# Dropped places and weights of the last lists, place by place on ScalarE

## The chip, the cores and the metric

The kernel runs on one core of a Trainium2 chip. The metric is the device time of one execution in microseconds, as the median of several runs. A core has five engines that run their own instruction queues and wait for one another by semaphores: TensorE (PE, with its weight load PEld), VectorE (DVE), ScalarE (ACT), GpSimd (POOL) and SyncE (SP). Here POOL does little else than issue indirect DMAs (gathers and scatters of rows), and SP issues the plain DMAs.

## The reference, cut to what matters

Sixteen graphs of 1024 nodes with 64 channels each, and a weighted adjacency matrix for each graph. Layer 0 is a dense product; layer 1 takes, for every node and channel, three quantiles over the node's neighbours:

```python
# layer 0
h = relu(layernorm(x));  x = x + matmul(adj / clip(sum(adj, 2), 1), h)
# layer 1
h = relu(layernorm(x))
adj_d = _dilate_adj(adj, mask)      # nodes with over 10 neighbours lose every (m+1)//2-th one,
                                    # in both directions of the edge
vals = where(adj_d > 0, h of the neighbour, big);  sv = sort(vals, axis=2);  m = number of valid ones
for tau, wt in zip([0.25, 0.5, 0.75], [0.25, 0.5, 0.25]):
    pos = tau * (m - 1)             # linear interpolation between floor(pos) and ceil(pos)
    agg += wt * (sv[floor(pos)] * (1 - frac) + sv[ceil(pos)] * frac)
out = h + agg
x = x + (relu(out @ W1 + b1) @ W2 + b2) * mask
```

The three quantiles together are a weighted sum over sorted places: each place k has one weight per node, which depends on m alone.

## The kernel before, in words

**Lists.** The kernel does not sort 1024 values for a node. It lists each node's neighbours (`listing`, `endings`), sorts the nodes by their number of neighbours into tiles of 128, and writes their records in that order to a table in DRAM (`srt`). The graphs are taken in four groups of four. In a group the tiles of equal list length form classes: 15, 10, 8, 7 (two tiles), 6, 5 (four), 4 (four), 3 (six), 2 (six) and 1 (five) neighbours (`CAPS`). A class is one `Job` with `n` places (the node itself is the first) and `T` tiles; with 15, 10, 8 and 6 neighbours `T` is 1. The longest lists of all graphs go into four jobs of 88, 28, 21 and 18 neighbours (`long_lists`); the first of them has the tag `l0` and is sorted in blocks as its gathers arrive.

**A job.** `Job.run` has POOL gather row by row: for place k an indirect DMA brings, for 128 nodes, the neighbour's 64 values and two marks into `A[:, k, t, :]` (tile `places`, or `lplaces` for a long list). Then `sort` works on VectorE. It compares the marks with the node's number (`rem`), which gives `gone`, 1 where the edge was dropped; from the keys and `gone` it gets `ok` and the number of valid neighbours, and from that the distances of the places from the three quantile positions (`counts`: `valid`, `q`, `u`, shown as `wu`). The values of gone neighbours are raised by 1e30, so that they sort behind all others:

```python
nc.vector.scalar_tensor_tensor(vals, gone..., HUGE, vals, op0=OP.mult, op1=OP.add)   # the drop
```

ScalarE then turns `u` into weights (`steps`: Abs, then Relu). `passes` does the sorting network: min and max of places, written to one of two copies, `A` (copy 0) or `other` (copy 1: PSUM for the short lists, tile `lother` in SBUF for the long ones). The last part is `weigh`: `w` is the sum of the three weights, and the sorted places are multiplied by it, into the tile `prod` for the short lists, in place for the long ones. `layers` then has PE add up the weighted places (matmuls with the identity into `pt`), ScalarE copy the sum out (`ot`), and PE, ScalarE and PE do W1, Relu (`hid`) and W2; VectorE adds the residual (`y`), and POOL scatters `y` to the output.

**Order.** The order on VectorE and POOL, and so on all engines, is fixed when the program is built. The steps are generators that yield an engine and a time from which they may go on; `Plan` keeps a clock for each engine with a price for every instruction, and always takes the step that may begin first, by its rank. `SLACK`, `LOOSE` and `LATE` are added to the times at which a result is thought to be there. `later` puts the passes of a list behind others while enough gathers are queued. So an edit of one step can move all later ones. Tiles have few buffers: 4 of `places`, 2 of `prod`, 1 of `other` and `lother`, 3 of `lplaces`. All planned instructions are recorded at one line, L240, so the rows of the profile are told apart by their tiles.

The edit lies in `sort` and `weigh`; `counts`, `steps`, `passes` and `layers` are as they were.

Of the kernel before, what the change touches and what calls it, by code (L numbers as in the profile page):

```python
# [14 lines left out]
AF = mybir.ActivationFunctionType  # L15
OP = mybir.AluOpType
AX = mybir.AxisListType

P = 128
# [4 lines left out]
HUGE = 1.0e30  # L24
# [57 lines left out]
def runs_of(left):  # L82

    left, runs = sorted(left), []
    while left:
        best = left[:1]
        for s in sorted({x - left[0] for x in left[1:]}):
            run = left[:1]
            while run[-1] + s in left:
                run.append(run[-1] + s)  # L90
            if len(run) > len(best):
                best = run
        runs.append((best[0], best[1] - best[0] if len(best) > 1 else 1, len(best), 1, 1))
        left = [x for x in left if x not in best]
    return runs
# [131 lines left out]
SLACK = 2.0  # L227
# [18 lines left out]
class Plan:  # L246
# [25 lines left out]
    def room(self, name, bufs):  # L272

        tiles = self.slots.get(name, ())
        if len(tiles) < bufs:
            return 0.0
        old = tiles[-bufs]
        return INF if self.users[old] else max(self.used.get(old, 0.0), self.ready.get(old, 0.0))

    def at(self, *tiles):  # L280
        return max(self.ready.get(t.tensor.name, INF) for t in tiles)
# [67 lines left out]
def kernel(  # L349
# [27 lines left out]
    with tc.manual_schedule(engines={mybir.EngineType.DVE, mybir.EngineType.Pool}):  # L377
        list_path(tc, x, adj, nodemask, w1, b1, w2, b2, out, go)
# [7 lines left out]
def list_path(ctx, tc, x, adj, nodemask, w1, b1, w2, b2, out, go):  # L386
    nc = tc.nc
    B, N, C = x.shape
# [5 lines left out]
    NG = len(GROUPS)  # L394
# [115 lines left out]
    plan = Plan(nc)  # L510
    plan.parts.update(tab.tensor.name for tab in tabs)
    nc = plan.nc
    new, free, room, at = plan.tile, plan.release, plan.room, plan.at
    always = lambda: 0.0
# [330 lines left out]
    class Job:  # L845
# [121 lines left out]
        def places(self, copy, run, shift=0):  # L967
            first, d1, n1, d2, n2 = run
            first += shift
            if copy == 2:  # L970
                return self.S[:, :, :C].unsqueeze(1)
            src = self.A if copy == 0 else self.other
            if n2 == 1:
                return src[:, first:first + d1 * (n1 - 1) + 1:d1, :, :C]
            one = src[:, first, 0, :C]
            row = src.shape[3]
            return bass.AP(
                tensor=one.tensor, offset=one.offset,
                ap=[one.ap[0], [d2 * row, n2], [d1 * row, n1], one.ap[1]],
            )  # L980
# [43 lines left out]
        def steps(self):  # L1024
            nc.scalar.activation(self.u, self.u, AF.Abs)
            nc.scalar.activation(self.u, self.u, AF.Relu, bias=wt0, scale=-QUANTILES[0][1])

        def merge(self):
            self.counts(self.ok)
            yield "ACT", lambda: at(self.u) + SLACK  # L1030
            self.steps()
            yield "DVE", always, self.later
            yield from self.passes(len(self.ops) - 1, self.landed)
            yield from self.weigh()

        def sort(self):
            n, T, pool, short, A, S = self.n, self.T, self.pool, self.short, self.A, self.S
            name, bufs = self.tag, self.bufs1
            rem = new(pool, [P, n - 1, T, 2], F32, name + "rem2", bufs)
            nc.vector.tensor_tensor(  # L1040
                rem, A[:, 1:, :, C:],
                self.node.unsqueeze(1).unsqueeze(3).to_broadcast([P, n - 1, T, 2]), OP.is_equal,
            )
            gone = new(pool, [P, n - 1, T], F32, name + "gone", bufs, users=1)
            nc.vector.tensor_tensor(gone, rem[:, :, :, 0], rem[:, :, :, 1], OP.max)
            ok = new(pool, [P, n - 1, T], F32, name + "ok", bufs)
            nc.vector.scalar_tensor_tensor(
                ok, self.keys.rearrange("p t k -> p k t"), 0.0, gone, op0=OP.is_gt,
                op1=OP.subtract,
            )  # L1050
            self.ops, self.count, self.copies = network(n, T * C, one=T == 1)
            self.counts(ok)

            vals = A[:, 1:, :, :].rearrange("p k t w -> p (k t) w")[:, :, :C]
            nc.vector.scalar_tensor_tensor(
                vals,
                gone.rearrange("p k t -> p (k t)").unsqueeze(2).to_broadcast(
                    [P, (n - 1) * T, C]
                ),
                HUGE, vals, op0=OP.mult, op1=OP.add,  # L1060
            )
            free(gone)
            yield "ACT", lambda: at(self.u) + SLACK
            self.steps()
            yield "DVE", lambda: max(
                room("prod", 2) if short else 0.0,
                room(name + "other", 1),
            ), self.later
            if short:
                Bt = self.Bt = new(ps_o, [P, 3 * HALF], F32, "other", 1, users=1)  # L1070
                self.other = Bt[:, :n * T * C].rearrange("p (k t c) -> p k t c", k=n, t=T)
            else:
                self.other = self.Bt = new(pool, [P, n, T, C], F32, name + "other", 1, users=1)
            self.done = {}
            yield from self.passes(0, plan.clock["DVE"])
            yield from self.weigh()

        def weigh(self):
            n, T, pool, short, A, S = self.n, self.T, self.pool, self.short, self.A, self.S
            name, bufs, Bt = self.tag, self.bufs1, self.Bt  # L1080
            u, count, copies, places = self.u, self.count, self.copies, self.places
            yield "DVE", lambda: at(u) + SLACK, self.later

            w = new(pool, [P, count, T], F32, name + "w", bufs)
            nc.vector.tensor_tensor(w, u[:, 0, :, :], u[:, 1, :, :], OP.add)
            nc.vector.scalar_tensor_tensor(w, u[:, 2, :, :], 2.0, w, op0=OP.mult, op1=OP.add)
            free(u)

            total = max(count + 1, 4)
            prod = None  # L1090
            if short:
                prod = new(pool, [P, T, total, C], F32, "prod", 2, users=1)
                if count + 1 < total:
                    nc.vector.memset(prod[:, :, count + 1:, :], 0.0)

            for copy in (1, 0):
                mine = [k for k in range(count) if copies[k] == copy]
                for run in runs_of(mine):
                    first, step, number = run[:3]
                    sl = slice(first, first + step * (number - 1) + 1, step)  # L1100
                    src = places(copy, run)
                    nc.vector.tensor_tensor(
                        prod[:, :, sl, :].rearrange("p t k c -> p k t c") if short else src, src,
                        w[:, sl, :].unsqueeze(3).to_broadcast([P, number, T, C]), OP.mult,
                    )
            if short:
                free(A)
                free(Bt)
                yield "ACT", lambda: at(S)
                nc.scalar.copy(prod[:, :, count, :], S[:, :, :C])  # L1110
                free(S)

                terms = [
                    [prod[:, t, k:min(k + 2, total), :].rearrange("p k c -> p (k c)")
                     for k in (0, *range(4, total, 2), 2)]
                    for t in range(T)
                ]
                plan.add(self.layers(terms, [prod]), self.urgent)
            else:
                terms = [[places(copies[k], (k, 1, 1, 1, 1))[:, 0, 0, :] for k in range(count)]  # L1120
                         + [S[:, 0, :C]]]
                plan.add(self.layers(terms, [A, Bt]), -1000)
# [354 lines left out]
    nc = tc.nc  # L1477
# [291 lines left out]
```

## Time and profile before

| what | value |
|---|---|
| median of 3 runs | 1457.18 us (1456.25 to 1458.25) |
| profiled execution | 1457.89 us, its span 1456.0 us |
| VectorE busy | 1214.5 us, 83% of the span |
| GpSimd busy | 960.6 us, 66% |
| TensorE busy | 745.0 us, 51%, at a mean granted clock of 0.703 |
| ScalarE busy | 579.9 us, 40% |
| DMA | 132.20 MB, 91 GB/s on average |

The profile is of one execution. The span runs from its first to its last instruction. A row names the line, the engine, the operation, and the tiles written and read; shapes are partitions x elements. "idle before" is the time that the engine stood still just ahead of the row, with what ended it; "issue" means that nothing which the profile shows was waited for. The first two thirds (up to about 950 us) are layer 0 and the first groups' lists, in which all engines have work. After that come the last group's lists and the long ones.

### The profile page before, as it was taken

Reading aid. Unit: us, or ns where it says so; the run is one execution under the profiler, and the core shown is the slowest. Engines: PE = TensorE matmul, PEld = TensorE weight load, DVE = VectorE, ACT = ScalarE, POOL = GpSimd, SP = SyncE. Lnnn points to the kernel's source line nnn. Section 1 sums busy time; section 2 is a strip of 40 time slices with the busy share of each in tenths; the row PEclk is TensorE's granted clock in tenths of the full one; section 3 lists DMA queues with packets and bytes.
Section 4 is the critical chain, followed back from the end, with each engine's and each line's share of the span. In section 5 each row is a group of like instructions: output and inputs, shape, how many; then the busy total and the mean of one; then the engine's idle time right before and its main releaser. Section 6 shows DMA issues by size and latency. Waiting matters only on the chain.

```text
span 1456.0 us, 14752 instructions
## 1 busy us (share of the span) xinstructions
PE 745.0 (51%) x3186; PEld 463.6 (32%) x3186; DVE 1214.5 (83%) x4039; ACT 579.9 (40%) x1747; POOL 960.6 (66%) x1120
## 2 busy tenths in 40 slices
PE   4777877345697566783666660002300262134674
PEld 2434434223345434352443430001200141134453
DVE  6868798997989968899766874868999979999885
ACT  7989978444656527672353830000000010001110
POOL 0132227777767887677778576577777877777754
PEclk9879998668697687895587775555555575558576
DMA  5445567524464416472232334121111111212100
GB/s 183 138 128 184 176 199 203 137 52 143 100 175 117 107 34 181 121 191 78 71 108 76 87 70 89 42 55 44 37 23 24 27 29 27 41 34 46 24 16 14
DMA packets 134589, 132.20 MB, mean 91 GB/s; under 512 B 100196, under 2 KB 102884, under 8 KB 134372
## 3 DMA queue, kind: packets, MB, share of 16 engines
q1 hardware_dynamic: 102972, 91.00, 21.8%
q0 software_dynamic: 31520, 40.19, 12.8%
q8 instruction: 27, 0.44, 0.1%
q14 instruction: 70, 0.57, 0.1%
HBM read 111.62 MB, written 23.61 MB: 93 GB/s over the span
## 4 chain that ended last, share of the span: by engine, by line
DVE 36%; POOL 22%; issue 11%; PE 10%; DMA 10%; ACT 9%; SPq 0%; DVEq 0%; POOLq 0%; ACTq 0%
POOL places L240 14%; DVE places L240 6%; PE ps_small L240 5%; PE pt L240 5%; DMA at<-in_adj_dram 5%; DVE lplaces L240 4%; DVE other L240 4%; DVE rec L240 4%; DMA places<-tab,idx 3%; POOL out_dram L240 3%; ACT sg L240 3%; DVE l0other L240 3%; POOL lplaces L240 2%; ACT ln_sq L240 2%; DVE sg L240 2%
## 5 line engine op out<-in xcount | busy, mean ns | idle before, releaser
L240 POOL DMA_INDIRECT places<-tab,idx x372 | 375.5, 1009 | 114.5 <-issue 106.7
L240 PE MATMUL pt<-ident,prod 128*128 128x128 f32 (+1 forms) x736 | 162.0, 383 | 389.8 <-DVE prod L240 325.0
L240 PE MATMUL ps_small<-att,h 128*65 128x512 f32 x512 | 254.3, 644 | 27.9 <-ACT att L240 9.4
L240 PEld LDWEIGHTS pt<-ident,prod 128*128 128x128 f32 (+1 forms) x736 | 131.6, 264 | 422.2 <-issue 250.6
L240 POOL DMA_INDIRECT srt<-row,to x128 | 130.3, 1018 | 179.4 <-ACT row L240 158.6
L240 PE MATMUL pt<-ident,at 128*128 128x128 f32 x1024 | 168.4, 309 | 65.9 <-ACT att L240 51.8
L240 DVE MAX8 rec<-sg 128x8 f16<-128x256 f16 x512 | 180.1, 414 | 4.4
L240 POOL DMA_INDIRECT lplaces<-whole,lidx x125 | 145.4, 1164 | 38.1 <-issue 36.9
L240 ACT ACTIVATE sg<-at 128x1024 f16<-128x1024 f32 x128 | 134.9, 1054 | 87.0 <-DMA at<-in_adj_dram 75.1
L240 PEld LDWEIGHTS pt<-ident,at 128*128 128x128 f32 x1024 | 130.0, 158 | 113.8 <-ACT att L240 77.6
L240 POOL DMA_INDIRECT places<-tab,last_idx x124 | 133.5, 1077 | 37.8 <-issue 35.7
L240 ACT ACTIVATE wu<-wu 128x39 f32<-128x39 f32 (+9 forms) x40 | 9.4, 235 | 354.2 <-DVE wu L240 354.0
L240 ACT COPY att<-pt 128x512 f32<-128x512 f32 x256 | 142.0, 583 | 18.9 <-PE pt L240 16.9
L240 DVE TENSOR_TENSOR sg<-sg,keyed 128x1024 f16<-128x1024 f16 x128 | 87.3, 682 | 48.3 <-ACT sg L240 48.3
L240 PEld LDWEIGHTS ps_small<-att,h 128*65 128x65 f32 x512 | 73.8, 150 | 164.5 <-issue 122.7
L240 ACT COPY ot<-pt 128x128 f32<-128x128 f32 (+3 forms) x56 | 22.4, 400 | 220.5 <-PE pt L240 220.4
L240 POOL DMA_INDIRECT out_dram<-y,nodes_i x93 | 94.0, 1010 | 22.3 <-issue 13.3
L240 PE MATMUL ps_small<-ot,w_sb 128*128 128x128 f32 (+3 forms) x112 | 50.8, 544 | 29.5 <-ACT ot L240 16.0
L240 DVE TENSOR_TENSOR places<-places,other 128x128 f32<-128x128 f32 (+6 forms) x160 | 56.3, 354 | 3.3
L240 PE MATMUL ps_small<-w_sb,hid 128*128 128x64 f32 x256 | 51.8, 343 | 7.1 <-ACT hid L240 6.8
L240 ACT ACTIVATE hid<-ps_small,b_sb 128x128 f32<-128x128 f32 (+2 forms) x56 | 28.2, 504 | 64.0 <-PE ps_small L240 63.9
L240 DVE TENSOR_TENSOR places<-other,places 128x128 f32<-128x128 f32 (+5 forms) x136 | 48.7, 365 | 1.7
(270 smaller groups left out, 1635.3 us busy)
## 6 DMA issues: line engine op xcount, KB each, us to landing
at<-in_adj_dram SPq DMA_DIRECT2D x128, 512.0 KB
places<-tab,idx POOLq DMA_INDIRECT x372, 2.6
whole<-tab SPq DMA_DIRECT2D x4, 1057.0 KB
tab<-row SPq DMA_DIRECT2D x16, 264.0 KB
xt<-in_x_dram SPq DMA_DIRECT2D x16, 256.0 KB
srt<-row,to POOLq DMA_INDIRECT x128, 3.4
lplaces<-whole,lidx POOLq DMA_INDIRECT x125, 2.5
places<-tab,last_idx POOLq DMA_INDIRECT x124, 2.5
```

Source lines behind the costliest of these rows:

```text
L240: ins = getattr(self._engine, op)(*args, **kwargs)
```

## The change

A new method, `helped`, says for a job whether ScalarE is to take part: jobs of the last group and the long lists other than the 88-place one, with one tile, where the planner's clock of ScalarE is less than 2 us ahead of VectorE's. For such a job the drop is done on ScalarE: `gone` is multiplied by 1e30, and each place gets its column of `gone` as a bias. In `weigh` each place that is to be weighted by copy 0 (for the long lists by both copies) is multiplied on ScalarE by its column of `w`. Both yield to the planner after every four places. The first pass of such a list waits for `A` plus `SLACK`.

```diff
+        def helped(self):
+            return (
+                self.g >= NG - 1 and self.tag != "l0" and self.T == 1
+                and plan.clock["ACT"] < plan.clock["DVE"] + 2.0
+            )
@@ sort
-            vals = A[:, 1:, :, :].rearrange("p k t w -> p (k t) w")[:, :, :C]
-            nc.vector.scalar_tensor_tensor(
-                vals,
-                gone.rearrange("p k t -> p (k t)").unsqueeze(2).to_broadcast(
-                    [P, (n - 1) * T, C]
-                ),
-                HUGE, vals, op0=OP.mult, op1=OP.add,
-            )
+            helped = self.helped()
+            if helped:
+                yield "ACT", lambda: at(gone) + SLACK
+                nc.scalar.mul(gone, gone, HUGE)
+                for t in range(T):
+                    for k in range(1, n):
+                        if (t or k > 1) and k % 4 == 1:
+                            yield "ACT", always
+                        val = A[:, k, t, :C]
+                        nc.scalar.activation(val, val, AF.Identity, bias=gone[:, k - 1, t:t + 1])
+            else:
...
             yield "DVE", lambda: max(
-                room("prod", 2) if short else 0.0,
+                at(A) + SLACK if helped else 0.0, room("prod", 2) if short else 0.0,
                 room(name + "other", 1),
             ), self.later
@@ weigh
+            helped = self.helped()
             for copy in (1, 0):
                 mine = [k for k in range(count) if copies[k] == copy]
+                if helped and (copy == 0 or not short):
+                    yield "ACT", lambda: at(w) + SLACK
+                    for e, k in enumerate(mine):
+                        if e and e % 4 == 0:
+                            yield "ACT", always
+                        for t in range(T):
+                            src = places(copy, (k, 1, 1, 1, 1))[:, 0, t, :]
+                            nc.scalar.activation(
+                                prod[:, t, k, :] if short else src, src, AF.Copy,
+                                scale=w[:, k, t:t + 1],
+                            )
+                    continue
...
-                yield "ACT", lambda: at(S)
+                if not helped:
+                    yield "ACT", lambda: at(S)
                 nc.scalar.copy(prod[:, :, count, :], S[:, :, :C])
```

More of the change, by code (lines that the diff above doesn't have):

```diff
@@ L1052, in sort @@
             self.counts(ok)
-            vals = A[:, 1:, :, :].rearrange("p k t w -> p (k t) w")[:, :, :C]
-            nc.vector.scalar_tensor_tensor(
-                vals,
-                gone.rearrange("p k t -> p (k t)").unsqueeze(2).to_broadcast(
-                    [P, (n - 1) * T, C]
-                ),
-                HUGE, vals, op0=OP.mult, op1=OP.add,
-            )
+            helped = self.helped()
[9 more added lines that the diff above has]
+            else:
+                vals = A[:, 1:, :, :].rearrange("p k t w -> p (k t) w")[:, :, :C]
+                nc.vector.scalar_tensor_tensor(
+                    vals,
+                    gone.rearrange("p k t -> p (k t)").unsqueeze(2).to_broadcast(
+                        [P, (n - 1) * T, C]
+                    ),
+                    HUGE, vals, op0=OP.mult, op1=OP.add,
+                )
             free(gone)
@@ L1094, in weigh @@
                     nc.vector.memset(prod[:, :, count + 1:, :], 0.0)
+            helped = self.helped()
             for copy in (1, 0):
                 mine = [k for k in range(count) if copies[k] == copy]
+                if helped and (copy == 0 or not short):
[8 more added lines that the diff above has]
+                                scale=w[:, k, t:t + 1],
+                            )
+                    continue
                 for run in runs_of(mine):
```

## The prediction

> **What bounds the kernel now.** I read the page's busy line, then the busy time by stretch, then who waited for whom on VectorE from 1151 us on, then the chain that ended last, and last the timeline of the final 22 us. 1151.3 us is where the first edited instruction starts (the 28-place drop below); the changed program's order is the same before it.
>
> ```profile
> PE 745.0 (51%) x3186; PEld 463.6 (32%) x3186; DVE 1214.5 (83%) x4039; ACT 579.9 (40%) x1747; POOL 960.6 (66%) x1120
> ```
>
> The 40% of ScalarE (ACT) is an average over two halves. By stretch (columns: span, then PE, PE load, DVE, ACT, POOL busy, granted clock, DMA share, GB/s):
>
> ```profile
> 1200.00:1250.00 50.00, 11.42 (x42) 9.30 (x41) 47.62 (x158) 3.01 (x11) 38.56 (x53) 0.51 0.16 32
> 1300.00:1350.00 50.00, 25.88 (x182) 23.29 (x181) 46.95 (x120) 4.04 (x11) 39.61 (x37) 0.74 0.21 38
> 1383.20:1440.50 57.30, 35.93 (x202) 27.68 (x202) 52.07 (x190) 7.61 (x18) 31.89 (x55) 0.74 0.05 17
> ```
>
> In the stage that is edited, VectorE (DVE) is at 94 to 95%, ScalarE at 6 to 13%. POOL's 39 of 50 us are gathers of 0.95 us with 0.30 us of issue between them, so POOL is full as well until its last gather ends at 1383.2. What VectorE waited for from 1151 us on:
>
> ```profile
> DVE rem L240 <- DMA places<-tab,idx: 9.5, 1, 9.5
> DVE y L240 <- PE ps_small L240: 6.7, 1, 6.7
> DVE rem L240 <- issue: 6.4, 3, 3.9
> DVE prod L240 <- PE pt L240: 3.5, 1, 3.5
> DVE rem L240 <- DMA places<-tab,last_idx: 0.6, 2, 0.3
> ```
>
> That is 20.0 us before the last list's weights (9.5 + 6.4 + 3.5 + 0.6) and 6.7 us after. All `rem` rows are waits for a gathered list, so two clocks run here: POOL's gathers, and VectorE's own queue. After 1385 the gathers are over and VectorE works off the long lists alone. The chain that ended last closes so:
>
> ```profile
> 1418.75 1.62 DVE y L240 x8
> 1435.67 1.25 DVE lplaces L240 x5
> 1440.39 5.12 PE pt L240 x32
> ```
>
> And the last list on VectorE (start, duration, instruction, idle before):
>
> ```profile
> 1438.70 0.17 DVE L240 TENSOR_TENSOR lw<-lwu 128x15 f32<-128x15 f32 x1
> ...
> 1439.11 1.09 DVE L240 TENSOR_TENSOR lother<-lother,lw 128x896 f32<-128x896 f32 x1
> 1440.12 0.21 DVE L240 TENSOR_TENSOR lplaces<-lplaces,lw 128x64 f32<-128x64 f32 x1
> ...
> 1447.26 0.28 DVE L240 SCALAR_TENSOR_TENSOR y<-ps_small,lS 128x64 f32<-128x64 f32 x1 [6.73 <-PE ps_small L240]
> ```
>
> From the weights' start at 1438.70 to `y` at 1447.26 is 8.56 us, of it 6.87 from PE's first matmul. The span then ends 8.7 us after `y`, with the output scatter at 1447.83.
>
> [...] `ln_sq`, 64 elements with one pointer, has 340 ns; five `h` with two pointers (433 ns each) take 1.77 us, so the step is (1.77 - 0.43) / 4 = 0.335, an overlap of 0.10. One pointer at 64 elements is thus 0.24 us a step (estimate). [...] the trace has two table loads, and no Identity. [...]
>
> **What is removed.** All seven candidate lists take the branch in the built program, at both places. From the groups kept apart by shape, drops: 28, 21, 18 places (long) 2.017, 1.550, 1.351; 15, 10, 8, 6 places 1.150, 0.817, 0.684, 0.549; sum 8.12. Weights: long 1.552 + 0.226, 1.291, 1.092 + 0.215; short 1.026 (13 places) and 0.215; sum 5.62. Fourteen instructions, 13.74 us of durations. In a full queue one starts about 0.08 before its forerunner ends (the 1.09 us one at 1439.11 is followed at 1440.12), so 13.74 - 14 x 0.08 = 12.6 us of VectorE's time go.
>
> **What is added.** On ScalarE 7 multiplies of `gone` (about 0.2), 106 drops and 68 weights: 174 x 0.24 + 1.4 = 43 us over 305 us in which ScalarE was busy 31. There is room. But it has to be in time. A drop of 15 places ends 0.4 + 0.2 + 15 x 0.24 = 4.2 us after its `rem`. Summing the old rows' times along VectorE's new order, the first comparison on that list stands 8.6 us of work after its `rem`; for the lists of 10, 8 and 6 places it is 15.9, 18.7 and 7.0 us against 3.0, 2.5 and 2.0; for the long ones over 45 us against at most 7.4. So no drop is waited for, and I price them at nothing; without that cover each costs its 2 to 7 us. `gone` itself, `wu` and the evictions (`ot`, `hid`) wait behind up to 28 drops, 6.7 us; each `y` on VectorE is placed later than that, by 5 us where it is tightest (the 12-place and 18-place lists' `y`, ahead of the last long list).
>
> **What moves.** The planner re-sorts every queue after 1151 us. POOL has the same instructions, but nine scatters (some 1.31 us each with their memset) now stand ahead of parts of the last list's five gathers, and its last gather is 16 instructions later. From the end of the 12-place list at 1376.0: five scatters 6.5, four gathers 5.1, four scatters 5.2, one gather: issued 1393.1, ended 1394.1, landed (1.8 later, as 1383.24 to 1384.97) at 1395.9, where it was 1385.0. The other lists' last gathers hold their places to within two instructions, so they land when they did (the eight-place list's come 32 earlier). SP issues the same small loads.
>
> Now VectorE against the landings, in sums of old durations from 1151.3 in the new order. The old `rem` of the five-place list came after 20.1 us of work, the new after 20.4: it waits 9.4 to 1181.1. Next, 15 places: work 38.3, ready 1199.0, landed 1200.9, wait 1.9. 10, 8, 14 and 6 places (51.8, 65.2, 108.4, 118.2): ready after landing. 20 places: 147.2, ready 1309.8 against about 1311, wait 1.2. 16 places: none. 18 places: 192.6, ready 1356.4 against 1359.45, wait 3.1. 12 places: 209.2, ready 1376.1 against 1377.9, wait 1.7. Last five places: 227.6, ready 1396.2 against 1395.9: none. Waits 17.3 instead of 20.0: the removed work partly becomes waiting for gathers (18 and 20 places), while the 3.5 us for `prod` should go, since its new place is some 8 us behind PE's last read. The last list's weights start after 253.0 us of work instead of 265.8 (11.4 removed before them, 1.35 us of `y` now stand after): 1151.3 + 253.0 + 17.3 = 1421.6; the same sum for before gives 1437.1 against the true 1438.7, small gaps I don't list, of which the landings absorb most; I take 1421.9. That is 16.8 earlier.
>
> The end gets longer. PE reads the `lplaces` term first, and ScalarE scales it last of 15: two sums 0.41, hand-over 0.1, 15 x 0.24 + 0.1 = 3.7, hand-over 0.1, PE to `y` 6.87, and another list's matmul put among these 0.4: 11.6 instead of 8.56, +3.0. `y` at 1433.5, its scatter at 1434; POOL's eight queued scatters from 1422 on end at about 1433, just ahead. Sum: -16.8 + 3.0 = -13.8. The profiled execution is 1457.89 us with a span of 1456.0; it would be 1444.1. Against the median of 1457.18 that is 1443.4; I say 1443.5.
>
> **Unknowns, both ends.** The ScalarE step: 0.24, at best 0.21 (`row<-rec`, 32 elements), at worst 0.43 with no overlap: -0.5 to +2.9 us at the end. Landings of the last five-place list: -1 to +6 (POOL mean gather 1.39, not 1.25, with its long ones). The `prod` and `y` waits: 0 to 4.
>
> **Rivals.** (A) as summed, -12 to -17: 0.68. (B) POOL's moved scatters become the wait: one of them stands at the queue's head for its `y`, and the last gathers land 5 us later still, VectorE waits at the last `rem` and ends later by the same; or PE's `prod` wait stays (3.5). For it: POOL is full. Against: those `y` are on VectorE by 1370, their scatters due at 1382 or later. -7 to -10, about 1449: 0.22. (C) Slower: the small ScalarE instructions cost far more than their rows, for instance a table load (1.28 us in this trace) at each change of function. At the end alone 15 x (p - 0.24) must exceed 13.8: it decides from p = 1.16 us. Against it: the built program has two table loads, as before. At 1.5 us a piece the end is 19 us longer, 1462: 0.04. (D) The gain is refilled by waits for gathers, nothing is left, 1457: for it, 9.5 of 20 us of waits are of this kind; against, after 1385 there are no gathers, and 55 us of VectorE's queue remain: 0.03. The rest, 0.03, is a gain over 17.
>
> **Numbers.** Likeliest 1443.5, its own range 1440 to 1446; with B's centre 1440 to 1450.5. Within 0.2% (2.9 us) is about what a measurement of this kernel can tell from no change. Faster 0.93 (A, B and the rest), same 0.03 (D), slower 0.04 (C).
>
> **What would show it.** Right: VectorE's busy time down by 13 to 14 us, ScalarE's up by about 174 x 0.34 = 60; seven `gone` rows on ScalarE, no third table load; no new VectorE wait for ScalarE; the last `lw` at about 1422 and PE's last run of 32 starting some 4.5 us after it. Wrong: VectorE waiting on `lplaces`, `places` or `y` from ScalarE or PE by more than 4 us, or a last `rem` after 1400.

## The result, and the profile after

The changed kernel takes 1442.55 us (median of four, 1442.01 to 1443.08), the kernel before 1457.41 us (median of four): a ratio of 0.9899, with a 95% interval of 0.9881 to 0.9916. The prediction was 1443.5 us. The profiled execution has a span of 1440.1 us where it was 1456.0, so 15.9 us less, and its own time is 1442.01 us. That profiled pair differs by 1.0 us more than the medians do. The twelve runs of the experiments below were measured in three groups, each with its own runs of the kernel before, which takes 1821 to 1834 us there, with engines standing still for reasons that no view names. The record names the chips of the groups as 0, 3 and 15, and none for the measurement above. I say "the normal chip" and "these chips" for short; whether the chip makes the difference, or something else, isn't known. Total times are compared only inside one group, and what is read from a trace is said each time. The ratios of these groups are made from the faster runs of both kernels alone (in the second group 9 of the 63 of the kernel before), so they aren't the quotients of the medians beside them, which are of all runs.

The busy line of the page:

```profile
PE 744.5 (52%) x3186; PEld 464.1 (32%) x3186; DVE 1202.7 (84%) x4025; ACT 621.0 (43%) x1928; POOL 958.0 (67%) x1118
```

VectorE has 14 instructions and 11.8 us less, ScalarE 181 instructions and 41.1 us more. The busy time by stretch, in the two stretches shown of before (columns: span, then PE, PE load, DVE, ACT, POOL busy, granted clock, DMA share, GB/s):

```profile
1200.00:1250.00 50.00, 11.77 (x42) 9.39 (x42) 48.00 (x169) 13.51 (x57) 40.45 (x53) 0.53 0.15 36
1300.00:1350.00 50.00, 27.70 (x179) 24.31 (x178) 47.36 (x137) 3.77 (x10) 38.84 (x39) 0.74 0.18 37
```

VectorE is still at 95 and 96%. The queue got shorter, not emptier. Who waited for whom on VectorE from 1151 us on:

```profile
DVE y L240 <- PE ps_small L240: 10.2, 2, 6.0
DVE rem L240 <- DMA places<-tab,idx: 5.7, 1, 5.7
DVE rem L240 <- DMA places<-tab,last_idx: 4.0, 1, 4.0
DVE rem L240 <- issue: 4.0, 2, 2.7
```

The wait for `prod` is gone, there is no wait for ScalarE, and the waits at a `rem` sum to 13.7 us. The chain that ended last closes with PE's last run (first fence), and the timeline of the last long list, rows picked (start, duration, instruction, idle before), shows how the end is reached:

```profile
1424.39 4.52 PE pt L240 x28
```

```profile
1418.50 0.17 DVE L240 TENSOR_TENSOR lw<-lwu 128x15 f32<-128x15 f32 x1
1418.92 3.45 ACT L240 ACTIVATE lother<-lother,lw 128x64 f32<-128x64 f32 x14 [8.50 <-DVE lw L240]
1422.27 0.33 ACT L240 ACTIVATE lplaces<-lplaces,lw 128x64 f32<-128x64 f32 x1
1422.66 0.69 PE L240 MATMUL pt<-ident,lplaces 128*64 128x128 f32 x2 [1.82 <-ACT lplaces L240]
1430.72 0.28 DVE L240 SCALAR_TENSOR_TENSOR y<-ps_small,lS 128x64 f32<-128x64 f32 x1 [6.00 <-PE ps_small L240]
```

Fourteen weight steps in 3.45 us, so (3.45 - 0.33) / 13 = 0.24 us each. PE starts with the place that ScalarE does last, 4.2 us after `lw`, and `y` follows 12.2 us after `lw`.

I split the stage the same way for both kernels, by VectorE's instructions: from the first `lok` of the 28-place list to the last `lw`. Gaps on VectorE of more than 0.3 us count as waits; the rest I call the net queue.

| us | before | after | difference |
|---|---|---|---|
| start of the stage (first `lok`) | 1150.5 | 1149.3 | -1.2 |
| net queue of the stage | 268.5 | 255.5 | -13.0 |
| waits in the stage | 19.7 | 13.7 | -6.0 |
| last `lw` to last `y` | 8.6 | 12.2 | +3.7 |
| last `y` to the end of the span | 8.7 | 9.4 | +0.6 |
| sum | | | -15.9 |

The first row is not the change's doing. Up to the 28-place list's drop, ScalarE, POOL and PE have the same instructions in the same order in both traces, and the four runs of the kernel before lie 2.0 us apart. Without it the sum is -14.7, next to the 14.9 by which the medians differ.

### The profile page after: what moved, and what is told of

Its sections match the earlier page's. It is cut to its first block, busy times and chain, and to the rows that moved or that the text cites. A ratio compares the mean times of both kernels' runs of the same rounds, so it can differ in the third digit from the quotient of the medians.

```text
span 1440.1 us, 14965 instructions
## 1 busy us (share of the span) xinstructions
PE 744.5 (52%) x3186; PEld 464.1 (32%) x3186; DVE 1202.7 (84%) x4025; ACT 621.0 (43%) x1928; POOL 958.0 (67%) x1118
## 3 DMA queue, kind: packets, MB, share of 16 engines
q0 software_dynamic: 31520, 40.19, 11.4%
## 4 chain that ended last, share of the span: by engine, by line
DVE 34%; POOL 25%; ACT 11%; issue 11%; PE 10%; DMA 9%; SPq 0%; DVEq 0%; POOLq 0%; ACTq 0%
POOL places L240 13%; POOL lplaces L240 8%; DVE places L240 7%; DVE other L240 5%; PE pt L240 5%; PE ps_small L240 5%; DMA at<-in_adj_dram 4%; DVE rec L240 4%; ACT sg L240 3%; POOL out_dram L240 2%; DMA places<-tab,idx 2%; ACT ln_sq L240 2%; ACT att L240 2%; DVE sg L240 2%; DVE lplaces L240 2%
## 5 line engine op out<-in xcount | busy, mean ns | idle before, releaser
L240 POOL DMA_INDIRECT lplaces<-whole,lidx x125 | 142.4, 1139 | 38.1 <-issue 36.9
L240 PEld LDWEIGHTS pt<-ident,at 128*128 128x128 f32 x1024 | 129.9, 158 | 115.5 <-ACT att L240 77.4
L240 POOL DMA_INDIRECT out_dram<-y,nodes_i x93 | 94.3, 1014 | 20.4 <-issue 14.0
L240 DVE TENSOR_TENSOR other<-places 128x256 f32<-128x256 f32 (+4 forms) x124 | 48.2, 389 | 2.0
```

The costliest lines, as they stand in the source:

```text
L240: ins = getattr(self._engine, op)(*args, **kwargs)
```

## The experiments

On these chips an execution takes about a quarter longer (1821 to 1834 us for the kernel before, against 1457). The net queue is not touched by this: the changed kernel itself has 255.7 us of it there, against 255.5. What grew is the gaps, from 13.7 to 83.0 us. So the table below gives the ratio to the kernel before of the same group, and what the trace says of VectorE's queue and of the tail (from the last `lw` to the last `y`). No experiment leaves any part of the computation out; some add neutral work.

| kernel | time, kernel before of the same group (us) | ratio (95%) | net queue | gaps | `lw` to `y` |
|---|---|---|---|---|---|
| removed work put back | 1797.9, 1820.8 | 0.986 (0.979 to 0.993) | 267.3 | 74.5 | 15.0 |
| the same, second group | 1826.8, 1831.6 | 1.008 (1.002 to 1.013) | 267.2 | 63.0 | 15.7 |
| the same, third group | 1833.4, 1834.0 | 1.002 (0.999 to 1.005) | 266.3 | 77.9 | 15.8 |
| changed kernel again | 1830.4, 1834.0 | 0.999 (0.996 to 1.001) | 255.7 | 83.0 | 14.5 |
| drops alone | 1805.1, 1820.8 | 0.989 (0.982 to 0.997) | 260.5 | 81.8 | 9.5 |
| the same, third group | 1831.3, 1834.0 | 0.997 (0.994 to 1.000) | 261.5 | 77.4 | 9.3 |
| weights alone | 1803.6, 1820.8 | 0.987 (0.978 to 0.997) | 262.7 | 73.6 | 14.6 |
| each drop twice | 1805.2, 1820.8 | 0.991 (0.988 to 0.993) | 256.7 | 79.6 | 14.1 |
| weights in PE's order | 1830.3, 1831.6 | 0.998 (0.993 to 1.002) | 255.7 | 64.1 | 14.8 |
| all lists of the last group | 1846.6, 1831.6 | 1.009 (1.006 to 1.012) | 246.5 | 74.9 | 14.7 |
| both of these | 1851.9, 1831.6 | 1.009 (1.007 to 1.012) | 246.0 | 97.0 | 16.9 |
| the same, third group | 1851.2, 1834.0 | 1.011 (1.003 to 1.018) | 246.3 | 82.6 | 17.8 |

The ratio of one and the same kernel (the first three rows) runs from 0.986 to 1.008 between groups (the quotients of its medians from 0.987 to 1.000). The part of the execution ahead of the stage, which no edit touches, takes 1424 to 1489 us in these twelve traces and 1149 to 1151 on the normal chip, so most of the added time, and of its scatter, lies outside what the edits change. A difference of a few us in the time can't be told here, and I don't tell it. The changed kernel itself was run in the third group alone.

### The removed work put back, order unchanged

```diff
+        def back(self, elements):          # neutral: col_f * 1 + 0, not priced by the planner
+            while elements > 0:
+                part = min(elements, N)
+                tc.nc.vector.scalar_tensor_tensor(col_f[:, :part], col_f[:, :part], 1.0,
+                                                  zeros[:, :part], op0=OP.mult, op1=OP.add)
+                elements -= part
@@ sort, ScalarE's branch
+                self.back((n - 1) * C)
@@ weigh, ScalarE's branch
+                    self.back(len(mine) * C)
```

> The changed kernel with the removed 12.6 us put back on VectorE: at each place where a drop or a weighting went to ScalarE, VectorE multiplies a constant tile by 1 over the same number of elements, which the planner isn't told of, so that its order on VectorE and POOL stays that of the changed kernel. Theory 1 (two clocks: VectorE's queue and the gathers; the new order let VectorE wait 13.7 us for gathers, and work put in front of a wait is swallowed by it): adding the old durations along the new order against the changed kernel's landings leaves about 5 us of waits, the last list's weights start 2.5 to 3.5 us later, 1445 to 1446 us. Theory 2 (VectorE is full, the gain is the removed work and nothing else): 12 us later, about 1454.5. A time near 1457 would say that the new order is worth nothing.

> The changed kernel in its own order, with a neutral VectorE instruction (a constant tile times one plus zero, in place) put at each place where the change took a drop or a weight product from VectorE, as many elements as the removed one had; ScalarE still does all 181 new steps. Theory (VectorE's queue is what the last stage costs, so the change is worth what it takes from that queue): some 13.7 us of durations come back, of which about 8.6 us is seen because VectorE's waits for the gathers shrink from 13.7 us to about 5 us and its `prod` wait doesn't return; last `lw` near 1421 us in an undisturbed profile against 1418.5, and a time of about 1445 to 1447 us. Rival 1 (all of it is the removed work, the order is worth nothing): back to 1454 to 1457 us. Rival 2 (the gain is the new order of gathers and scatters, the removed work is worth nothing): 1442 to 1443 us.

> The changed kernel with neutral VectorE work of the removed sizes put back at the removed places, order unchanged. To be read against the changed kernel of the same call. Theory (the gain is what VectorE's queue lost, less the gather waits that open): 2.5 to 5 us slower than it (1445 to 1447 us where the kernel before takes 1457). Rival 1 (all of the gain is the removed work): 12 to 15 us slower, level with the kernel before. Rival 2 (all of it is the new order): within 1 us of it. Where the chip is in the state of the first eight runs, differences below 5 us can't be told.

The rivals are about how much of the gain is the work and how much the new order. POOL's order, and that of VectorE's planned instructions, is the changed kernel's; on ScalarE and PE a few instructions trade places. The work comes back in 19 pieces of at most 1024 elements, 14.5 us of durations where 13.7 were removed. The busy lines of the changed kernel and of this one, both of the third group, in that order:

```profile
PE 802.2 (44%) x3186; PEld 494.9 (27%) x3186; DVE 1205.7 (66%) x4025; ACT 624.3 (34%) x1928; POOL 938.2 (51%) x1118
```

```profile
PE 793.8 (43%) x3186; PEld 491.1 (27%) x3186; DVE 1217.3 (67%) x4044; ACT 624.5 (34%) x1928; POOL 943.3 (52%) x1118
```

VectorE gets 11.6 us back, and its net queue in the stage grows from 255.7 to 266.3, 267.2 and 267.3 us. The kernel before has 268.5. So of the 12.8 to 13.0 us that the queue lost, 10.6 to 11.6 come back with the work (the prediction has 11.4 removed ahead of the last `lw`; the nineteen pieces have about 11.8 there, durations less 0.08 each), and 1.2 to 2.2 are left for the new order (1.35 by the `y` rows that now stand behind it). In the last stretch, from the second last long list's `lw` to the last one's, there is no gap in any of these traces: 19.4 us for the changed kernel on both kinds of chip, 20.8 to 20.9 with the work put back. There the work counts in full. How much of the time would come back can't be read: no wait for a gather is left in the stage on these chips, so the waits that should have shrunk from 13.7 to 5 us are not there to shrink. In the third group the medians differ by 3.0 us, the ratios by 0.003, which is 5.7 us, and the two intervals (0.9958 to 1.0013 and 0.9988 to 1.0047) overlap, so the time decides between none of the three outcomes. The split of the time between work and waits stays open; that of the queue is shown.

### The changed kernel again

> The changed kernel itself, unedited, as the yardstick of the other three on the same chip. Where the kernel before takes 1457 us: 1442 to 1443.5 us (ratio 0.990). Where the chip is in the state of the first eight runs (kernel before at 1820 to 1832 us, engines standing still in stretches with no releaser in sight): the gain of VectorE's queue holds (ratio 0.988 to 0.992) if those standstills fall alike on both kernels; if they go by the number of instructions, the 167 more instructions of the changed kernel eat part or all of it (0.995 to 1.005).

Ratio 0.9986, and the interval holds 1: on that chip the change is worth nothing that can be measured. Its queue is as short as on the normal chip, so the gain went elsewhere. The two longest waits in its trace of the stage and the tail, and then one of "weights alone", where the drops are on VectorE:

```profile
DVE w L240 <- ACT wu L240: 14.3, 3, 7.4
DVE y L240 <- PE ps_small L240: 12.5, 2, 8.3
```

```profile
DVE w L240 <- ACT wu L240: 14.3, 2, 11.3
```

VectorE waits 14.3 us for the quantile weights (`wu`) that ScalarE makes; on the normal chip it waited for ScalarE not once in the stage. In the changed kernel `wu` stands behind the drops, but the wait is just as long with the drops on VectorE, so it can't be put down to them. What the change does cost there is the tail: 14.5 us, 5.0 to 5.2 longer than with the weights on VectorE (9.5 and 9.3 in "drops alone"), where the normal chip had +3.7. There was also no gather wait to save. The queue's 12.8 us less some 5.1 of tail would leave a gain of 7.7, which is the edge of the interval (0.9958 of 1834). What became of the rest stays open, because there is no profile of the kernel before on such a chip.

### Drops alone, weights alone

```diff
@@ weigh (drops alone)                @@ sort (weights alone)
-            helped = self.helped()
+            helped = False
```

> Drops on ScalarE, weights on VectorE as before. Theory 1: 7.6 us of the 12.6 are gone from VectorE, and the tail after the last weights is the old 8.6 us instead of 12.2; along its own order the last weights start at about 1420.7, so the last y at 1429.3 and a time of about 1441, 1 to 1.5 us below the changed kernel. Theory 2 (only removed work counts): 5.0 us above it less 3 for the tail, 1444.5.

> The changed kernel with the drops alone on ScalarE; all weights stay on VectorE, as before. Theory (two clocks): the short lists' weights are small (1.2 us) and the long ones' 4.4 us stand after the last gather, where each is seen, but the tail from the last `lw` to the last `y` is 3.6 us shorter; 1442 to 1445 us where the kernel before takes 1457. Rival (each part counts by its durations, 8.1 of 13.7 us): 1448 to 1449 us.

> Weights on ScalarE, drops on VectorE as before. Theory 1: along its order, which is nearly that of the kernel before, the last weights start at about 1425, and up to 3.5 us later if VectorE's wait for the buffer prod is still there; with the long tail of 12.2 the time is 1448.5 to 1452.5. Theory 2: 7.6 us above the changed kernel, 1450. Both lie together here; what tells is whether this part alone is worth less than its 5.0 us less the tail's 3.

The times don't tell them apart (0.989 and 0.997; 0.987). The queue does: with the drops alone it is 260.5 and 261.5 us, 7.0 to 8.0 below that of the kernel before on the normal chip, where the prediction's durations give 8.12 - 7 x 0.08 = 7.6. With the weights alone it is 262.7, 5.8 below. There the five products ahead of the last `lw` give 5.62 - 1.31 - 5 x 0.08 = 3.9, and three `y` rows have moved behind it, some 0.6 more: 4.5, so 1.3 us of it isn't accounted for. Together 12.8 to 13.8, in the changed kernel 12.8 to 13.0: the parts add to within 1 us. And the price is in the weights: the tail is 9.5 and 9.3 us with the drops alone, 14.6 with the weights alone.

### Each drop twice

```diff
                         nc.scalar.activation(val, val, AF.Identity, bias=gone[:, k - 1, t:t + 1])
+                        tc.nc.scalar.activation(val, val, AF.Identity, bias=zero_f)
```

> After every drop ScalarE does a second pass over the same place (adds zero), 106 more instructions that the planner isn't told of. Theory 1: ScalarE's queue is covered, also at double length (the tightest list, 15 places, is ready 7.8 us after its rem and first used after 8.6), so VectorE shows no new wait for ScalarE and the time stays within 1 us of the changed kernel's 1442.5. Rival (the drops on ScalarE are already on the path): 1 to 4 us per list, 1446 or more, with waits of VectorE at the first comparison of a list.

The question is how much cover the drops have. The only row of a VectorE wait that names them, of the whole execution (L1071 is the line of the second pass):

```profile
DVE other L240 <- ACT places L1071: 1.1, 1, 1.1
```

106 more steps on ScalarE, and one wait of 1.1 us, at the first comparison of the 15-place list. Doubled, the 15-place list's drops would end 0.4 + 0.2 + 30 x 0.24 = 7.8 us after its `rem`, against 8.6 us of VectorE work, so the cover is nearly used up where it is tightest, and the wait comes at that list. That no drop is waited for in the changed kernel, with half the steps, is thus not a near miss, as far as this chip can tell, on which both engines stand still as well.

### Long lists' weights in PE's order

```diff
                 if helped and (copy == 0 or not short):
+                    if not short:
+                        mine = range(count) if copy else []
@@
-                            src = places(copy, (k, 1, 1, 1, 1))[:, 0, t, :]
+                            src = places(copies[k], (k, 1, 1, 1, 1))[:, 0, t, :]
```

> The changed kernel, with the weights of a long list multiplied on ScalarE in the order of the places, in which TensorE's chain of additions also takes them, and not first the one copy and then the other. Theory (the tail from the last `lw` to the last `y` is ScalarE's 28 steps of 0.24 us ahead of the first matmuls that need the late ones): TensorE's last chain starts with ScalarE and follows it, and ends about 3.4 us sooner; but POOL's eight queued scatters end at 1429.2 us in the profile of after, so at most about 1.8 us of it is seen: 1440.5 to 1441.5 us. Rival (POOL's queue alone sets the end): 1442.5 us, nothing gained.

The last list has fifteen such steps, not the 28 of the expectation. PE's last chain in the changed kernel on such a chip, whose last `lw` starts at 1803.14, and then in this one, whose last `lw` starts at 1806.22, with the next instruction of ScalarE (rows picked):

```profile
1807.29 0.69 PE L240 MATMUL pt<-ident,lplaces 128*64 128x128 f32 x2 [1.82 <-ACT lplaces L240]
1808.96 4.99 PE L240 MATMUL pt<-ident,lother 128*64 128x128 f32 x26
1813.79 0.38 PE L240 MATMUL pt<-ident,lS 128*64 128x128 f32 x2
```

```profile
1807.03 0.43 PE L240 MATMUL pt<-ident,lplaces 128*64 128x128 f32 x2 [0.58 <-DVE y L240]
1808.71 2.82 PE L240 MATMUL pt<-ident,lother 128*64 128x128 f32 x12
1813.51 0.38 PE L240 MATMUL pt<-ident,lS 128*64 128x128 f32 x2
1818.61 0.26 ACT L240 COPY ot<-pt 64x128 f32<-64x128 f32 x1 [8.04 <-remote]
```

The mechanism is there: PE starts 0.8 us after `lw` instead of 4.2, and its chain ends 7.7 us after `lw` instead of 11.0, so 3.4 us sooner as expected. But ScalarE's copy of the sum starts 4.7 us after the chain's end (1818.61 against 1813.89), where it is 1.4 us in the changed kernel there and 0.1 us on the normal chip. ScalarE stood still, and the tail is 14.8 us, no shorter. POOL's queue of scatters was over at 1817.0, ahead of the last `y` at 1820.99; with ScalarE on time `y` would have come at about 1816 (2.0 us after the copy, as in the changed kernel there), and the queue would have been the limit, as I had expected. Whether that is worth 1.8 us on a normal chip wasn't seen.

### All lists of the last group, and both edits

```diff
-                self.g >= NG - 1 and self.tag != "l0" and self.T == 1
+                self.g >= NG - 1 and self.tag != "l0"
```

> The changed kernel, with ScalarE also taking the drops and weights of the last group's lists that have more than one tile (85 more drop steps, 30 more weight steps). Theory (VectorE's queue is the bound, and ScalarE has room): VectorE's last products about 5 us sooner (adding up the order with the durations of the profile of after gives a last `lw` at about 1412 to 1414 us against 1418.5), waits for gathers up from 13.7 to about 18.5 us; time 1436 to 1439 us. Rival 1 (gathers are now the bound: every us taken from VectorE is waited for): 1441 to 1443 us. Rival 2 (ScalarE becomes the bound, each step waited for): above 1444 us.

> Both edits together: long lists' weights on ScalarE in the order of the places, and the last group's lists of more than one tile on ScalarE too. If the gains add (the one shortens the tail, the other what comes ahead of it): 1434 to 1438 us, and faster than either alone by 1 us or more. If POOL's queue of scatters at the end sets the time, no faster than the better of the two alone: within 0.5 us of it.

> The changed kernel plus both edits: long lists' weights on ScalarE in the order of the places, and the last group's lists of more than one tile on ScalarE too. Where the kernel before takes 1457 us: 1434 to 1440 us, that is 3 to 8 us faster than the changed kernel, with the last `lw` some 4 us earlier and the stretch from it to the last `y` some 2 to 3 us shorter than 12.2. In the state of the first eight runs: slower than the changed kernel by 1% or so, if each added ScalarE instruction is paid for there (115 more, of which VectorE then waits for some).

Slower than the kernel before by 0.9% (0.6 to 1.2), and with both edits by 0.9 and 1.1% (by the medians of all runs 0.8, 1.1 and 0.9%). VectorE's queue is another 9.2 to 9.7 us shorter, so the first half of the theory holds. The second, that ScalarE has room, isn't so simple. Waits on VectorE in the stage, rows picked, first with all lists, then with both edits in the third group:

```profile
DVE other L240 <- ACT places L240: 29.9, 2, 18.6
DVE w L240 <- ACT wu L240: 11.5, 1, 11.5
```

```profile
DVE lother L240 <- remote: 17.2, 1, 17.2
DVE other L240 <- ACT places L240: 12.9, 2, 11.0
DVE prod L240 <- PE pt L240: 7.5, 1, 7.5
```

Now VectorE waits for the drops themselves (`places` from ScalarE), up to 18.6 us at once. That is not ScalarE's work filling up: it is busy 95 of the stage's 321 us. The drops stand in its queue behind copies of a sum (`ot`) that could not go on, as the trace with all lists has it (the last long wait is the 18.6, the other the remaining 11.2):

```profile
1695.76 0.26 ACT L240 COPY ot<-pt 64x128 f32<-64x128 f32 x1 [72.98 <-PE pt L240]
1751.83 0.58 ACT L240 COPY ot<-pt 128x512 f32<-128x512 f32 x1 [14.18 <-remote]
```

The planner also moves the ends of several lists behind the last long list: fifteen `y` rows come after the last `lw` instead of nine, with both edits the tail is 16.9 and 17.8 us, and `prod` is waited for again. With all lists, ten scatters on POOL are still to come at the last `y` instead of one, and the span ends 17.7 us after it instead of 8.4. From the first `lok` to the last `lw` that trace is not slower than the changed kernel's on such a chip (321.5 against 338.7 us); from the last `lw` to the end it is 9.6 us longer. So the outcome of my second rival, above 1444 us, may fit, but its cause, each step waited for, isn't what is seen. On a chip without the standstills it may be otherwise, and that stays open. No version here is shown to beat the changed kernel.

## Why the prediction was right, step by step

**What bounds the stage.** Right: VectorE was full before (94 to 95% busy) and is full after (95 and 96%), and the end moved by its queue.

**The removed work.** Right: up to the last `lw` the prediction had 11.4 us of removed work, 1.35 of `y` moved behind it, together 12.8, and 1.3 of small gaps; the net queue lost 13.0 on the normal chip and 12.8 elsewhere, and 10.6 to 11.6 of it come back with the work. Only the small gaps were not there. The overlap of 0.08 us at each of the fourteen borders belonged into the sum, as the prediction had it.

**Busy times.** VectorE "down by 13 to 14" was -11.8, ScalarE "up by 60" was +41.1. Both were stated as sums of durations, while the page counts overlapping instructions once: 174 x 0.24 = 42 and the 12.6 of the queue were the right figures, and both stood in the prediction.

**The ScalarE step.** 0.24 us for weights (above), and the drops the same: eighteen in 4.40 us. That is the prediction's estimate from `ln_sq` and `h`, whose 340 ns and overlap of 0.10 us fit too: the groups of these steps have a mean of 334 or 335 ns, and in a row they overlap by 0.09 to 0.10. The trace has two table loads of 1.28 us, as before, and no third. Rival C is out.

**No drop is waited for.** Right, with room to spare (each drop twice). On the chips of the experiments `wu` was waited for, with the drops on VectorE too, and with all lists the drops as well, behind a ScalarE that stood still.

**The waits for gathers.** This is the term that was most mis-sized: "the other lists' last gathers hold their places to within two instructions, so they land when they did". They hold their places but land earlier. I said 17.3 us of waits (9.4, 1.9, 1.2, 3.1, 1.7); it was 13.7 (5.7, 2.7, 1.3, 4.0, and none). The first one makes the difference: that `rem` starts at 1176.6 instead of 1181.1, 4.5 us sooner, of which 1.2 is the earlier start of the stage. The other 3.3 us are POOL's. Its gathers beside VectorE's wide instructions, in the timeline of before:

```profile
1151.31 2.02 DVE L240 SCALAR_TENSOR_TENSOR lplaces<-lgone,lplaces 128x1792 f32<-128x1792 f32 x1
1151.99 2.19 POOL L240 DMA_INDIRECT lplaces<-whole,lidx  x1 [0.30 <-issue]
1155.20 1.35 DVE L240 TENSOR_TENSOR prod<-places,w 128x1152 f32<-128x1152 f32 x1
1155.75 1.62 POOL L240 DMA_INDIRECT lplaces<-whole,lidx  x1 [0.30 <-issue]
1159.92 1.55 DVE L240 SCALAR_TENSOR_TENSOR lplaces<-lgone,lplaces 128x1344 f32<-128x1344 f32 x1
1160.17 2.12 POOL L240 DMA_INDIRECT lplaces<-whole,lidx  x1 [0.30 <-issue]
```

And the same three gathers of POOL's queue after:

```profile
1150.76 0.98 POOL L240 DMA_INDIRECT lplaces<-whole,lidx  x1 [0.30 <-issue]
1153.30 0.95 POOL L240 DMA_INDIRECT lplaces<-whole,lidx  x1 [0.30 <-issue]
1157.06 0.95 POOL L240 DMA_INDIRECT lplaces<-whole,lidx  x1 [0.30 <-issue]
```

The three gathers of before each start while a wide VectorE instruction runs, and end 0.82 to 0.85 us after that instruction's end (1154.18 after 1153.33, 1157.37 after 1156.55, 1162.29 after 1161.47). Over POOL's instructions of the stage up to that `rem`, what they take above 0.95 us sums to 3.84 us before and 0.59 after: 3.25 us, the size of the gap. Of it, 2.4 us stand beside the two removed drops. Most of the rest is luck of order: the product of 1152 elements is still there after, from 1152.05 to 1153.43, but one gather starts 0.01 us ahead of it and the next 0.13 us before its end, and neither is held. So the two removed drops paid twice, 2.02 and 1.55 us on VectorE and 1.2 us each on POOL. The trace of before showed gathers held so, and I had used the mean gather instead. Up to POOL's last gather it nearly cancels (21.4 us above 0.95 before, 20.4 after), because after the change more of POOL's indirect DMAs are held (45 over 1.1 us instead of 32), each for less; it counts where a list waits for its last gather.

**The last five places.** I said landed at 1395.9 and not waited for; their last gather ends at 1390.5 instead of 1394.1, and their `rem` starts at 1392.5 without a wait. Rival B's wait did not come, and the `prod` wait went as said. Rival D, that the gain is refilled by waits for gathers, is out too: those waits became fewer.

**The tail.** Said +3.0 to 11.6 us, measured 12.2 (+3.7). ScalarE's part was right: its last weight ends 4.1 us after `lw`, against 4.2. PE to `y` took 8.1 instead of 7.3: another list's second matmul pair (`ps_small` at 1423.70) stands among the first terms too. After `y`, 0.6 us more that I did not follow up.

**Sum.** Said -13.8 for the span, measured -15.9, so -2.1 off: start -1.2, queue +1.1 (13.0 instead of 14.1 with the small gaps), waits -3.3, tail +0.7, after `y` +0.6. The median fell by 14.9; the prediction had put the fall at 13.7. That it came within 1 us is partly luck: the waits were off by 3.3 us, the tail, the end and the queue by 2.4 the other way, and the start of the stage is no part of the change.

## What to carry to other kernels

Where one engine's queue is full and another's nearly empty, a product that takes the full one 1.1 us is worth moving even if the idle one needs fifteen steps of 0.24 us for it, as long as its result is due later than that. Price the queue (starts, not durations), and look for the one place, here the last list, where nothing covers it. Here VectorE's products and drops with both inputs in SBUF also held up POOL's gathers, to 0.82 us after their own end, so ask of each that is removed whether a gather that somebody waits for stands beside it. And measure such a gain more than once and elsewhere: here the queue got 13 us shorter in every measurement, and the time did not.

## What the runs showed of the hardware

**Gathers and scatters held by VectorE ended 0.82 us after it.** In the stages of before and after, 97 indirect DMAs of POOL start inside a `tensor_tensor` or `scalar_tensor_tensor` of VectorE with both inputs in SBUF, more than 0.04 us after its start and at least 0.25 us ahead of its end. All 97 take over 1.0 us, and 95 of them end 0.80 to 0.88 us after VectorE does, 0.82 in the middle. Of 22 that start likewise beside an instruction with an input in PSUM, 21 take 1.0 us or less, and so do 22 of the 25 that start within 0.04 us of VectorE's start with both inputs in SBUF. The same product as in the fence of before above, but from `other`, which is in PSUM, stood beside a gather that took 0.95 us:

```profile
1323.17 1.49 DVE L240 TENSOR_TENSOR prod<-other,w 128x1280 f32<-128x1280 f32 x1
1323.88 0.95 POOL L240 DMA_INDIRECT places<-tab,last_idx  x1 [0.30 <-issue]
```

The other way round no block is seen: 502 VectorE instructions with two SBUF inputs, of forms that occur more than once, start in the first 0.8 us of such a DMA, and none takes over 0.05 us longer than the shortest of its form.

**Standstills of issue.** The same VectorE instructions with nothing between them, in the timeline of the changed kernel on the normal chip and of "each drop twice" on one of the others:

```profile
1146.05 0.24 DVE L240 TENSOR_REDUCE l0valid<-l0ok 128x1 f32<-128x88 f32 x1
1146.32 0.15 DVE L240 TENSOR_SCALAR l0valid<-l0valid 128x1 f32<-128x1 f32 x1
1146.51 0.16 DVE L240 TENSOR_TENSOR l0q<-taus,l0valid 128x3 f32<-128x3 f32 x1
```

```profile
1422.24 0.24 DVE L240 TENSOR_REDUCE l0valid<-l0ok 128x1 f32<-128x88 f32 x1
1425.67 0.15 DVE L240 TENSOR_SCALAR l0valid<-l0valid 128x1 f32<-128x1 f32 x1 [3.20 <-remote]
1427.07 0.16 DVE L240 TENSOR_TENSOR l0q<-taus,l0valid 128x3 f32<-128x3 f32 x1 [1.24 <-DVE l0valid L240]
```

Durations are equal to the hundredth; the starts are 1.4 to 3.4 us apart instead of 0.2 to 0.3. In that trace such gaps come again and again from 1412.4 to 1446.7 us, and from 1577.5 to 1590 there are none, as in the 19.4 us of the last list. ScalarE and PE show the like: in the same trace ScalarE's copies `att` wait 117.4 us for "remote" and PE's matmuls into `pt` 182.4 us for "issue", and the changed kernel on the normal chip has neither row. No view names what is waited for. The two DMA queues that carry instructions moved as much on both kinds of chip (1.04 MB for the changed kernel on the normal chip, 1.05 with the removed work put back in the second group, 0.1% of the DMA engines' time for each queue), so more fetching is not what differs. Inside each group the kernels with the most instructions in the stage have the highest ratios, which would fit a cost for each instruction; but in the first group the intervals overlap, and with all lists the end of POOL's queue is another reason, so it stays open.
